# Moving a value projection and splitting norm steps inside context attention

## The chip, the cores and the metric

The kernel runs on one core of a Trainium2 chip. The metric is the device time of one execution in microseconds (us); lower is better. All numbers below are us unless marked otherwise.

## The reference

One transformer block on `x` (2 x 1024 tokens x 256) with a context of 2 x 154 tokens x 192, everything in float32:

```python
h = _layernorm(x, ln1_g, ln1_b)
x = _attention(h, h, sa_wq, sa_wk, sa_wv, sa_wo, sa_bo) + x
h = _layernorm(x, ln2_g, ln2_b)
x = _attention(h, cond_emb, ca_wq, ca_wk, ca_wv, ca_wo, ca_bo) + x
h = _layernorm(x, ln3_g, ln3_b)
p = h @ ff_w1 + ff_b1
a, gate = (p[..., :D_FF], p[..., D_FF:])
h = a * jax.nn.gelu(gate, approximate=False) @ ff_w2 + ff_b2
return h + x
```

Attention has 16 heads of 64. The change touches context attention (the second one) and the norms that run beside it: the second norm (`ln2`) of batch 1 and the third norm (`ln3`) of batch 0.

## The kernel before

The program is one stream of instructions for each engine, in an order written out by hand. Nothing reorders it: each engine takes its instructions as they were emitted, and semaphores join the engines.

The work has three stages: self attention, context attention, and the gated feed-forward layer. In context attention a **unit** is one pair of heads of one batch. There are 16, unit 0 to 15; 0 to 7 are batch 0. A unit's 1024 tokens are taken in three **slots**, of 3, 3 and 2 tiles of 128 tokens. The loop over `c` (48 values) walks through them; `ui, n = divmod(c, 3)` gives unit and slot.

Each slot does the following, in order:

- `cross_first`: the scores `sc` on TensorE (64-row tiles, since a head has 64 features), their maxima on VectorE (`neg`), then exponentials on ScalarE (`p`, with their sums in `den`).
- `flush(stores)` before the exponentials emits copies that were held back from the slot before. `flush(lates)` emits the reciprocal (`rden`, VectorE) and the weighting by it (`p`, GpSimdE) for the slot before.
- `cross_drain`: two 32x32 block transposes of the weights on VectorE (`pT_ca`), for the slot two back.
- The slot's own share. Slot 0 has the cross values `poc` of the unit two back (`cross_values`, 32-row tiles, into two banks of the pool `mm_tile` and two of `sum_tile`), and VectorE and ScalarE copy them out (`o_ca`). Slot 1 has the query projection `pq` of the next unit (`cross_queries`, two `mm_tile` banks, 64-row tiles; ScalarE copies `q_ca`). Slot 2 has the output projection: pieces `py` of two token tiles each, added into the residual `x` by VectorE. Most units have two pieces, one ahead of and one behind the norm step of that slot.

Each of the two pools has two banks, given out in turn. So the first `mm_tile` bank taken after a query projection is the one that the first of the two query copies frees.

**Context values.** Every second unit (2, 4, ... 14) projects the context values of its own and the next unit with `context_values`: `pv`, two matmuls of 96 rows, in the trace four passes. ScalarE copies the result to `own_v`. SP's queue then writes it to memory (`vd`) and reads it back in another layout (`v_ca`). The function `back` and the list `later`, of which two entries are emitted at the end of a slot, set when that happens. In the kernel before, `pv` is emitted in slot 1, behind the queries, in a `sum_tile` bank.

**Norms beside the attention.** `norm_beside(kind, b)` puts the steps of a norm in the list `side`; `run_work` takes at most one of them in a slot. A norm has four kinds of function: `stats` (VectorE, two instructions for each of the eight token tiles), `deviation` (GpSimdE, two small ones for a pair of tiles), `normalize` (one small VectorE instruction, `off`, and two on GpSimdE, `xn`), and `turn` (TensorE transposes into a bank `ph`, then stores of `hT` on VectorE). For the two norms here a step `k` takes two tiles:

```python
for fns, first in ((turn, 3), (stats, 0), (deviation, 1), (normalize, 2)):
    for i, fn in enumerate(fns):
        t = i if fns is stats else 2 * i + 1
        lag.setdefault(first + t // n, []).append((fn, fns is turn))
```

So with `n = 2` steps 0 to 2 hold no `turn`; step 3 holds the first `turn`, the second `normalize`, the third `deviation` and the last two `stats`; step 4 has no `stats`, step 5 no `deviation`, and step 6 the last `turn` alone. A step with a `turn` needs a bank, and `run_work` in context attention gives one in slot 2 only; the other steps may go in any slot. `norm_beside("ca", 1)` is called in slot 0 of unit 2, `norm_beside("ff", 0)` in slot 0 of unit 11. In the kernel before, steps 0, 1 and 2 therefore run in the three slots of units 2 and 11, and steps 3 to 6 in slot 2 of the four units that follow (3 to 6, and 12 to 15).

GpSimdE also adds biases (`ca_bo`) and, in the last units, sums of feed-forward weights (`w1s`, `wf`) in these slots.

Of the kernel before, what the change touches and what calls it, by code (L numbers as in the profile page):

```python
# [18 lines left out]
def tile_transformer_block(ctx: ExitStack, tc: tile.TileContext, a: dict, out: bass.AP):  # L19
# [4 lines left out]
    B, S, D = x.shape  # L24
# [73 lines left out]
    for n in names:  # L98
        k = n_of[n]
# [204 lines left out]
    def tile_order(kind):  # L304

        if kind == "ff":
            return list(range(NT))
        return [t for i in range(NT // 2) for t in (i, NT // 2 + i)]

    def narrow(kind, b):  # L310

        return kind == "sa" or kind == "ca" and b < B - 1
# [13 lines left out]
    def norm_beside(kind, b):  # L326

        after = {"sa": None, "ca": "sa", "ff": "ca"}[kind]
        stats, deviation, normalize, turn = norm_pieces(kind, b)
        n = 1 if narrow(kind, b) else 2
        lag = {}
# [4 lines that stand above are left out]
        for k in range(NT // n + 3):  # L339
            tiles = tile_order(kind)[k * n:(k + 1) * n]  # L340
            needs = [(after, b, half, t) for half in range(NQ) for t in tiles if after]

            def step(fns=lag[k]):
                done = [fn() for fn, _ in fns]
                return next((fn for fn in done if fn), None)

            side.append((any(turns for _, turns in lag[k]), needs, step))
        if not narrow(kind, b):
            side.append((False, (), lambda: add_biases(kind, b)))

# [129 lines left out]
    def out_order(kind):  # L480

        return [t for t in tile_order("ff" if kind == "ca" else "ca") if t % 2 == 0]
# [73 lines left out]
    side, lates = [], []  # L556
# [3 lines left out]
    def run(piece):  # L560
        done = piece()
        if done is not None:
            (adds if getattr(done, "adds", False) else stores).append(done)

    def flush(queue):
        for fn in queue:
            fn()
        queue.clear()

    def run_work(n, n_side, bank=None, n_sum=0):  # L570

        while n > 0 and work:
            n -= work[0].banks
            run(work.pop(0))
        for _ in range(min(n_side, len(side))):
            needs_bank, needs, fn = side[0]
            if needs_bank and not bank and n <= 0 or not added.issuperset(needs):  # L580
                break
            if needs_bank and not bank:
                n -= 1
            spare["bank"] = bank or mm_tile
            run(fn)
            side.pop(0)
        for i in range(min(max(n, 0) + n_sum, len(outs))):
            spare["out"] = mm_tile if i < n else sum_tile
            run(outs.pop(0))

    def out_pieces(kind, b, half, tiles):
        outs.extend(lambda t=t: out_piece(kind, b, half, t) for t in tiles)

    units = [(b, pr) for b in range(B) for pr in range(NPAIR)]
# [227 lines left out]
    def context_values(b, pr, bank=mm_tile):  # L822

        v = vs["ca", b, pr // 2] = pt_.tile([P, NB, VC], F32, tag="V", name=f"v_ca{b}_{pr}")
        pv = bank(f"pv_ca{b}_{pr}")
        for c in range(2):
            nc.tensor.matmul(
                pv[:, :VC], lhsT=ctxT[:, c, b * TP:b * TP + P],  # L830
                rhs=wsl["ca", pr, "v"][:, c, :], start=(c == 0), stop=(c == 1),
            )

        def store():
            own = one.tile([P, VC], F32, tag="own_v", name=f"own_v{b}_{pr}")
            nc.scalar.copy(own, pv[:, :VC])
            later.insert(0, lambda: nc.sync.dma_start(out=vd[b, pr][:P, :], in_=own))

            def back(a0):
                for a4 in range(a0, a0 + 2):  # L840
                    nc.sync.dma_start(
                        out=v[a4 * KB:(a4 + 1) * KB, :, :],
                        in_=vd[b, pr].rearrange("(n p) d -> p n d", p=KB))

            later.insert(2, lambda: back(0))
            later.insert(3, lambda: back(2))

        return store
# [367 lines left out]
    with tc.manual_schedule():  # L1216
# [61 lines left out]
        for p in range(SA):  # L1278
# [11 lines left out]
            ui, n = divmod(p, 2 * SH)  # L1290
# [26 lines left out]
        for c in range(CA):  # L1317
            if c == 0:
                pTc["ring"] = pt_.tile(
                    [P, 2 * NK, QH // 2], F32, tag="pT", name="pT_ca"  # L1320
                ).rearrange("p a b -> p (a b)")[:, :3 * 2 * NB * NT * KB].rearrange(
                    "p (u n j q) -> p u n j q", u=3, n=NB, j=2)
            if c == SH:
                out_pieces("sa", B - 1, NQ - 1, out_order("sa"))
                w1, w2, parts = hold_gated()
                add_biases("ca", 0)
                others = later[:] + [lambda: None] * (len(parts) - len(later))
                later[:] = [fn for pair in zip(parts, others) for fn in pair] + others[len(parts):]
            ui, n = divmod(c, len(CG))
            nxt = units[ui + 1] if ui + 1 < NU else None  # L1330
            if n == 0:
                cross_beside(ui)
            elif n == 1 and 1 <= ui < NU - 2:
                load_weights("ca", units[ui + 2][1], "q")
            elif n == 2 and nxt and ui:
                load_weights("ca", nxt[1], "v")
            flush(adds)
            between = None
            if c < 2:
                if c == 0:  # L1340
                    turn_group(SA - 3, 1)
                reciprocals(SA + c - 2)
                factors(SA + c - 2)
            then = cross_first(c)
            if c < 2:
                weighted(SA + c - 2, 0)
                weighted_beside(SA + c - 2, 1)
                if c == 0:
                    slot[SA - 1]["dd"] = differences(SA - 1, slot[SA - 1]["st"])
                    between = lambda: softmax_join(SA - 1)  # L1350
            flush(stores)
            flush(lates)
            if n == 0 and ui > 1:
                own, between = cross_values(ui - 2, [mm_tile] * 2 + [sum_tile] * 2)
                lates.append(then(between))
                own()
            else:
                lates.append(then(between))
            if c < 2:
                turn_group(SA + c - 2, 0)  # L1360
                turn_group(SA + c - 2, 1)
            cross_drain(c)
            if c == 0:
                run(lambda: self_values(2 * NU - 2, 1))
            elif c == 1:
                run(lambda: cross_queries(*units[2]))
            elif c in (2, 3):
                run(lambda: self_values(2 * NU - 1, c - 2))
            elif n == 0:
                run_work(0, 1)  # L1370
            elif n == 1:

                spare["turned"] = True
                if ui == 1 or not nxt:
                    run_work(2, 0)
                else:
                    run(lambda: cross_queries(*nxt))
                    if ui % 2 == 0:
                        run(lambda: context_values(*units[ui], sum_tile))
                run_work(0, 1)  # L1380
            else:
                run_work(0, 0, n_sum=1)
                flush(adds)
                run_work(0, 1, mm_tile)
                flush(stores)
                if ui > 1:
                    run_work(0, 0, n_sum=1)
                if ui and ui % HP == 0:
                    load_out("ca", *divmod(ui // HP - 1, NQ))
            if c == 0:  # L1390
                load_out("sa", B - 1, NQ - 1)
            for _ in range(min(2, len(later))):
                later.pop(0)()
            if c == CA - 16:
                weighted = [fn for n in range(4) for fn in weight_sums(n)]
            if CA - 16 <= c < CA - 4:
                weighted.pop(0)()
            elif c >= CA - 3:
                for n in {CA - 3: (4,), CA - 2: (5, 6), CA - 1: (7,)}[c]:
                    weight_sums(n)[0]()  # L1400
            if c == CA - 5:
                token_sums(0)
# [78 lines left out]
```

## Time and profile before

| | |
|---|---|
| median of 3 runs | 1078.59 (1078.13 to 1078.92) |
| the profiled execution | 1078.65, of which the span is 1076.9 |
| TensorE busy | 1065.6 of the span |
| VectorE, ScalarE, GpSimdE busy | 875.2, 651.0, 765.4 |

A row of a timeline gives the start in us from the span's start, the duration, the engine, the line of the kernel, the operation, what it writes and reads, tile sizes on TensorE (rows*columns), shapes, how many instructions were merged into the row, and in brackets the idle time before it with the engine that ended it. PE is TensorE's matmuls, PEld its weight loads, DVE VectorE, ACT ScalarE, POOL GpSimdE, SPq a queue of transfers. A float32 matmul of the program shows as two passes. Ends of matmuls are modelled, so the distance from one row's start to the next is a better measure than the duration. In a table of windows each line gives the stretch, its length, the busy time and instruction count of PE, PEld, DVE, ACT and POOL, then the granted clock of TensorE, the busy share of the transfer engines and their GB/s.

### The profile page before, as it was taken

Reading aid. Unit: us, or ns where it says so; the run is one execution under the profiler, and the core shown is the slowest. Engines: PE = TensorE matmul, PEld = TensorE weight load, DVE = VectorE, ACT = ScalarE, POOL = GpSimd, SP = SyncE. Lnnn points to the kernel's source line nnn. Section 1 sums busy time; section 2 is a strip of 40 time slices with the busy share of each in tenths; the row PEclk is TensorE's granted clock in tenths of the full one; section 3 lists DMA queues with packets and bytes.
Section 4 is the critical chain, followed back from the end, with each engine's and each line's share of the span. In section 5 each row is a group of like instructions: output and inputs, shape, how many; then the busy total and the mean of one; then the engine's idle time right before and its main releaser. Section 6 shows DMA issues by size and latency. Waiting matters only on the chain.

```text
span 1076.9 us, 45967 instructions
## 1 busy us (share of the span) xinstructions
PE 1065.6 (99%) x19060; PEld 712.3 (66%) x19060; DVE 875.2 (81%) x1283; ACT 651.0 (60%) x2081; POOL 765.4 (71%) x1600
## 2 busy tenths in 40 slices
PE   8999999999999999999999999999999999999998
PEld 6545657567565565566665655567766677788998
DVE  5789999998989989999989998978766777654554
ACT  5666767667666666666776666666566555242221
POOL 2677777778777787777777777768665687488774
PEclk9999999999999999999999999999999999999999
DMA  3232122111111111211211211135323221000000
GB/s 95 63 91 63 46 47 46 33 43 30 41 40 33 43 43 29 53 43 24 53 24 33 53 24 38 24 103 131 97 57 83 68 58 41 1 10 11 21 11 30
DMA packets 99234, 50.56 MB, mean 47 GB/s; under 512 B 30218, under 2 KB 97810, under 8 KB 99026
## 3 DMA queue, kind: packets, MB, share of 16 engines
q1 hardware_dynamic: 97698, 46.96, 18.0%
q8 instruction: 150, 2.46, 1.0%
q10 hardware_dynamic: 1328, 0.66, 0.2%
q14 instruction: 58, 0.48, 0.1%
HBM read 35.25 MB, written 3.41 MB: 36 GB/s over the span
## 4 chain that ended last, share of the span: by engine, by line
PE 91%; POOL 3%; DVE 2%; DMA 1%; ACT 1%; issue 1%; SPq 1%; DVEq 0%; POOLq 0%; ACTq 0%
PE s L493 19%; PE po L547 19%; PE py_sa L467 5%; PE py_ca L467 5%; PE pv_sa L393 5%; PE pq_ca L362 5%; PE pq_sa L362 5%; PE pk_sa L362 5%; PE sc L867 4%; PE poc L932 4%; PE pb L1037 3%; PE pf L1161 3%; PE pa L1037 2%; PE pc L1037 2%; PE pf L1200 1%; DMA st<-st 1%
## 5 line engine op out<-in xcount | busy, mean ns | idle before, releaser
L613 POOL TENSOR_SCALAR p<-p,rd,ee 128x512 f32<-128x512 f32 x508 | 387.4, 773 | 91.4 <-DVE rd L605 88.1
L508 ACT ACTIVATE p<-s,st 128x512 f32<-128x512 f32 x512 | 345.9, 687 | 175.5 <-DVE st L502 169.7
L502 DVE TENSOR_REDUCE st<-s 128x2 f32<-128x1024 f32 x256 | 308.8, 1207 | 51.1 <-issue 20.4
L640 DVE STREAM_TRANSPOSE pT<-p 128x1024 f32<-128x1024 f32 x256 | 302.4, 1219 | 1.5 <-POOL p L613 1.5
L493 PE MATMUL s<-k_sa,q_sa 64*32 64x512 f32 x4096 | 256.1, 591 | 2.4 <-ACT p L508 1.6
L547 PE MATMUL po<-pT,v_sa 64*32 64x256 f32 x8192 | 239.5, 376 | 0.9 <-ACT p L885 0.9
L547 PEld LDWEIGHTS po<-pT,v_sa 64*32 64x32 f32 x8192 | 177.5, 106 | 71.4 <-issue 26.2
L493 PEld LDWEIGHTS s<-k_sa,q_sa 64*32 64x32 f32 x4096 | 83.5, 106 | 101.0 <-issue 52.7
L885 ACT ACTIVATE p<-sc,neg 128x154 f32<-128x154 f32 x256 | 96.9, 401 | 74.9 <-DVE rden L893 74.4
L896 POOL TENSOR_SCALAR p<-p,rden 128x154 f32<-128x154 f32 x256 | 97.4, 402 | 61.7 <-DVE rden L893 61.2
L508 ACT ACTIVATION_READ_ACCUMULATOR p<-s,st 128x1 f32 x512 | 103.4, 202 | 0.0
L526 POOL TENSOR_TENSOR dd<-st 128x8 f32<-128x8 f32 x128 | 25.9, 202 | 73.5 <-DMA st<-st 69.7
L872 DVE TENSOR_REDUCE neg<-sc 128x6 f32<-128x924 f32 (+1 forms) x48 | 48.0, 1000 | 31.0 <-PE sc L867 30.9
L393 PEld LDWEIGHTS pv_sa<-sa_wv,hT_ln 64*128 64x128 f32 x1024 | 58.5, 188 | 14.2 <-issue 9.2
L393 PE MATMUL pv_sa<-sa_wv,hT_ln 64*128 64x128 f32 x1024 | 61.7, 275 | 0.0
L467 PE MATMUL py_ca<-ca_wo,o_ca 128*128 128x256 f32 x256 | 60.8, 385 | 0.0
L467 PE MATMUL py_sa<-sa_wo,o_sa 128*128 128x256 f32 x256 | 59.8, 386 | 0.0
L467 PEld LDWEIGHTS py_sa<-sa_wo,o_sa 128*128 128x128 f32 x256 | 47.2, 190 | 18.0 <-ACT v_sa L402 5.9
L362 PE MATMUL pq_ca<-hT_ln,ca_wq 64*128 64x512 f32 (+1 forms) x352 | 58.2, 589 | 0.0
L362 PE MATMUL pk_sa<-hT_ln,sa_wk 64*32 64x512 f32 x960 | 57.1, 590 | 0.0
L362 PE MATMUL pq_sa<-hT_ln,sa_wq 64*32 64x512 f32 (+1 forms) x976 | 56.7, 586 | 0.0
L885 ACT ACTIVATION_READ_ACCUMULATOR p<-sc,neg 128x1 f32 x256 | 55.3, 216 | 0.0
(132 smaller groups left out, 1442.6 us busy)
## 6 DMA issues: line engine op xcount, KB each, us to landing
v_sa<-v_sa SPq DMA_DIRECT2D x32, 256.0 KB, 3.8
st<-st SPq DMA_DIRECT2D x510, 1.0 KB, 1.8
v_ca<-vd SPq DMA_DIRECT2D x32, 160.0 KB, 3.1
sa_wq<-in_L_xattn_sa_wq_dram SPq DMA_DIRECT2D x32, 128.0 KB, 3.2
sa_wk<-in_L_xattn_sa_wk_dram SPq DMA_DIRECT2D x32, 128.0 KB, 3.2
sa_wv<-in_L_xattn_sa_wv_dram SPq DMA_DIRECT2D x32, 128.0 KB, 3.2
ca_wq<-in_L_xattn_ca_wq_dram SPq DMA_DIRECT2D x32, 128.0 KB, 3.4
wf<-in_L_xattn_ff_w_dram SPq DMA_DIRECT2D x12, 256.0 KB, 5.3
```

Source lines behind the costliest of these rows:

```text
L362: nc.tensor.matmul(pq[r][f:f + m, at:at + n], lhsT=wt[own, c, f:f + m], rhs=h[own, c, t0:t0 + n], start=(c == 0), stop=(c == NH - 1), tile ...
L393: nc.tensor.matmul(pv[r][:, i * P:(i + 1) * P], lhsT=h[own, c, i * P:(i + 1) * P], rhs=wt[own, c, :], start=(c == 0), stop=(c == NH - 1), ...
L467: nc.tensor.matmul(py[:, e * D:(e + 1) * D], lhsT=o[:, i, (t + e) * P:(t + e + 1) * P], rhs=wo[kind, b, g][:, i, :], start=(i == 0), stop= ...
L493: nc.tensor.matmul(sc[a4 * KB:(a4 + 1) * KB, j, :], lhsT=q[r, c:c + KB], rhs=k[r, h * HB:(h + 1) * HB], start=True, stop=True, tile_positi ...
L502: nc.vector.tensor_reduce(st[:, 0, 0, i, :], sc, AX.X, ALU.max, negate=True)
L508: nc.scalar.activation(pr[:, j, :], sc[:, j, :], AF.Exp, bias=st[:, 0, 0, i, j:j + 1], accum_out=st[:, 0, 1, i, j:j + 1],)
L547: nc.tensor.matmul(po[a2][d:d + KB, :QH // 2], lhsT=v[r, t, e, d:d + KB], rhs=pT[r, d // DH * NK + n, :], start=(t == 0 and e == 0), stop= ...
L613: nc.gpsimd.tensor_scalar(pr[:, j, :], pr[:, j, :], v["rd"][:, c:c + 1], v["ee"][:, 0, c:c + 1], op0=ALU.mult, op1=ALU.mult,)
L640: nc.vector.transpose(halves[h][:, :, c:c + KB], slot[p]["members"][i].rearrange("p j (n k) -> p (j n) k", k=KB))
L885: nc.scalar.activation(pr_[:, j, i, :T], sc[:, j, i * T:(i + 1) * T], AF.Exp, bias=neg[:, j, i:i + 1], accum_out=den[:, j, i:i + 1],)
L896: nc.gpsimd.tensor_scalar(pr_[:, j, i, :T], pr_[:, j, i, :T], rden[:, j, i:i + 1], 1.0, op0=ALU.mult, op1=ALU.mult,)
L1037: nc.tensor.matmul(into[:, :BT], lhsT=lhs, rhs=wh[pair][i], start=first, stop=True, skip_group_check=True)
```

## The change

For the two norms named above each step with a `turn` is cut in two: the `turn` alone, and then the rest of the step as an entry of its own in `side`. The `turn` keeps slot 2; the rest, which needs no bank, is taken in the next slot, slot 0 of the following unit. The first step 3 now runs its `turn` in slot 2 of unit 3 (unit 12) and its `stats`, `deviation` and `normalize` in slot 0 of unit 4 (unit 13), and so on.

`context_values` is emitted in slot 2 of the same units, between the two output pieces and ahead of the `turn`, in an `mm_tile` bank; before it was in slot 1, in a `sum_tile` bank. Its copy to `own_v` is emitted at the end of slot 2, behind that slot's exponentials on ScalarE; before it was ahead of them. The order of transfers on SP's queue is the same as before, and so are the number and kind of all instructions.

```diff
-            def step(fns=lag[k]):
+            def step(fns):
                 done = [fn() for fn, _ in fns]
                 return next((fn for fn in done if fn), None)

-            side.append((any(turns for _, turns in lag[k]), needs, step))
+            parts = [lag[k]]
+            if kind == "ca" and b == B - 1 or kind == "ff" and b < B - 1:
+                parts = [[f for f in lag[k] if f[1] == turns] for turns in (True, False)]
+            for fns in parts:
+                if fns:
+                    side.append(
+                        (any(turns for _, turns in fns), needs, lambda fns=fns: step(fns)))
...
                 else:
                     run(lambda: cross_queries(*nxt))
-                    if ui % 2 == 0:
-                        run(lambda: context_values(*units[ui], sum_tile))
                 run_work(0, 1)
             else:
                 run_work(0, 0, n_sum=1)
                 flush(adds)
+                if ui and ui % 2 == 0:
+                    run(lambda: context_values(*units[ui]))
                 run_work(0, 1, mm_tile)
                 flush(stores)
                 if ui > 1:
```

## Prediction

> **What bounds the kernel now.** I read the page first, then a table of windows over the context-attention stage, cut where each unit's cross values (`poc`) start, then the timelines of TensorE, VectorE, ScalarE and GpSimdE inside it.
>
> ```profile
> span 1076.9 us, 45967 instructions
> PE 1065.6 (99%) x19060; PEld 712.3 (66%) x19060; DVE 875.2 (81%) x1283; ACT 651.0 (60%) x2081; POOL 765.4 (71%) x1600
> PE 91%; POOL 3%; DVE 2%; DMA 1%; ACT 1%; issue 1%; SPq 1%; DVEq 0%; POOLq 0%; ACTq 0%
> ```
>
> TensorE is busy for 99% of the span and carries 91% of the chain that ended last. A change counts only if it alters the sum of TensorE's steps or makes TensorE wait. All that the diff moves lies in units 2 to 14 of context attention. The windows (length, then PE, PEld, DVE, ACT and POOL busy) show what one unit costs:
>
> ```profile
> 740.28:753.14 12.86, 12.86 (x151) 9.72 (x149) 10.68 (x30) 7.89 (x38) 12.11 (x34) 1.00 0.98 228
> 753.14:767.42 14.28, 14.28 (x154) 9.71 (x152) 10.38 (x23) 8.05 (x37) 10.33 (x27) 1.00 0.19 53
> 767.42:779.79 12.37, 12.37 (x151) 8.80 (x149) 9.76 (x21) 7.69 (x36) 7.89 (x22) 1.00 0.59 154
> 779.79:793.41 13.62, 13.62 (x154) 9.38 (x153) 9.56 (x20) 8.07 (x37) 6.29 (x19) 1.00 0.16 45
> 793.41:805.33 11.92, 11.92 (x146) 8.40 (x144) 8.28 (x16) 7.72 (x36) 8.68 (x23) 1.00 0.37 79
> 805.33:818.52 13.19, 13.19 (x151) 9.00 (x149) 8.28 (x16) 8.07 (x37) 9.36 (x24) 1.00 0.14 42
> 869.80:882.46 12.66, 12.66 (x151) 9.13 (x149) 9.68 (x20) 7.68 (x36) 10.36 (x27) 1.00 0.27 67
> ```
>
> A plain unit (7) takes 11.92. With transposes (5) it is 12.37, with a value projection (8) 13.19, with both (6) 13.62. So the projection costs 1.27 (13.19 - 11.92) or 1.25 (13.62 - 12.37), the transposes 0.45. Units 3, 4 and 13 exceed their kind by 0.49, 0.66 and 0.29: those are waits.
>
> **The projection, moved.** TensorE in unit 6, and in unit 5, which has no projection:
>
> ```profile
> 783.02 3.60 PE L362 MATMUL pq_ca<-hT_ln,ca_wq 64*128 64x512 f32 x16
> 786.55 1.13 PE L829 MATMUL pv_ca<-ca_wv,ctxT 96*128 96x256 f32 x4
> 787.61 0.80 PE L867 MATMUL sc<-kT,q_ca 64*128 64x154 f32 x8
> 788.33 1.99 PE L467 MATMUL py_ca<-ca_wo,o_ca 128*128 128x256 f32 x8
> 790.16 0.60 PE L280 MATMUL ph_ln<-ident,xn_ln 128*128 128x128 f32 x4
> 790.60 1.89 PE L467 MATMUL py_ca<-ca_wo,o_ca 128*128 128x256 f32 x8
> 792.42 1.06 PE L867 MATMUL sc<-kT,q_ca 64*128 64x154 f32 x12
> ```
> ```profile
> 770.66 3.60 PE L362 MATMUL pq_ca<-hT_ln,ca_wq 64*128 64x512 f32 x16
> 774.09 0.69 PE L867 MATMUL sc<-kT,q_ca 64*128 64x154 f32 x8
> 774.71 1.99 PE L467 MATMUL py_ca<-ca_wo,o_ca 128*128 128x256 f32 x8
> 776.54 0.60 PE L280 MATMUL ph_ln<-ident,xn_ln 128*128 128x128 f32 x4
> ```
>
> Today `pv` stands between queries and scores, both in 64-row tiles, and itself uses 96 rows. From start to start, queries to the next step take 3.53 with `pv` behind them and 3.43 without; `pv` takes 1.06; scores to output tile take 0.72 behind it and 0.62 without. That adds up to 1.26, as the windows say. How much of it is matmul? Eight passes of 256 columns take 1.83 in `py`, which is also entered from 64 rows.
>
> ```profile
> 786.55 0.73 PEld L829 LDWEIGHTS pv_ca<-ca_wv,ctxT 96*128 96x128 f32 x4 [0.76 <-DVE pT_ca L912]
> 789.95 0.57 PEld L280 LDWEIGHTS ph_ln<-ident,xn_ln 128*128 128x128 f32 x4
> L829 PE MATMUL pv_ca<-ca_wv,ctxT x32: 379/379/483, 693.3 to 890.0; 96*128 96x256 f32 x32
> L467 PE MATMUL py_ca<-ca_wo,o_ca x256: 379/379/483, 748.1 to 930.7; 128*128 128x256 f32 x128
> ```
>
> Both operations have passes of 379 ns and first ones of 483 (a pass overlaps the next, so these are not pitches). The excess of 0.10 is a weight load in the open: the first load of `pv` starts with its matmul at 786.55, while that of `ph`, between two 128-row groups, starts 0.21 ahead of its matmul. One pass is therefore (1.83 - 0.10) / 8 = 0.216, four are 0.86, and about 0.4 of `pv` is the price of leaving 64-row tiles and coming back. Between the two output tiles nothing is left and come back to. The transposes already there prove it: 0.44 in the timeline (790.16 to 790.60), 0.45 in the windows, no surcharge. Saving: 1.27 - 0.86 = 0.41 in three units without transposes (2, 8, 10) and 1.25 - 0.86 = 0.39 in four with them (4, 6, 12, 14), together **2.8**.
>
> The trace has no 96-row pass next to a 128-row one. If 96 against 128 costs as much as 96 against 64, the saving is 0; if it costs nothing, 2.8, or 2.9 at most. I take 2.8, because `pv` and `py` have the same durations, first passes included, and differ only in unused rows. The Trainium skill (TensorEngine Tiling (Array Packing), Key Properties and Available Configurations) says that a change of tiling mode drains TensorE, and lists row tilings of 128, 64 and 32 only. By it 96 rows would run as the 128-row mode and the sum would be 2.8; no run here shows that.
>
> What is queued behind the moved `pv`: transposes, second output tile, next scores, cross values. Its new wait is for the bank of the first query copy. In unit 5 the two copies start at 4.41 after the queries (row below), so the first is done at 4.96; `pv` would come at 774.71 - 770.66 + 1.83 = 5.88. Cover 0.9: no cost in units 6 to 14. On ScalarE the copy of `pv` now stands behind four exponentials, 1.5 us later (below), and its bank is next wanted by `poc`, which starts 10.4 after the queries (793.41 - 783.02); in unit 5's rhythm the copy is done by about 7.4 (4.41 + 1.1 + 1.5 + 0.4). On SP's queue the write of `own_v` and all behind it (value read-backs, query weights) wait as much longer; values are needed two units later, weights one, so nothing shows.
>
> **The norm steps, moved.** Before, statistics, deviation and normalization ran in slot 2 with the transposes. In unit 3:
>
> ```profile
> 750.70 0.42 DVE L240 BATCH_NORM_STATS2 st_ln<-x 128x6 f32<-128x256 f32 x1
> 751.82 1.36 DVE L291 TENSOR_SCALAR hT_ln<-ph_ln,cols 128x128 f32<-128x128 f32 x4
> 753.10 0.68 DVE L474 TENSOR_TENSOR x<-py_ca,x 128x512 f32<-128x512 f32 x1
> 753.14 3.08 PE L932 MATMUL poc<-pT_ca,v_ca 32*64 32x256 f32 x80
> ```
>
> Statistics and offset take 1.12 on VectorE (750.70 to 751.82) ahead of the transposes' stores and the add that frees a bank for `poc`. The add ends at 753.78, 0.64 after `poc` starts. That is unit 4's excess of 0.66, and unit 13 loses its 0.29 the same way. After the change that VectorE work starts after `poc`, so both go: **0.95**. The statistics of tiles still ahead of any transpose (units 2 and 11) do not move, nor do their waits.
>
> They come back in slot 0, in front of the maxima of slot 1. Unit 2 shows today what that does:
>
> ```profile
> 732.05 3.60 PE L362 MATMUL pq_ca<-hT_ln,ca_wq 64*128 64x512 f32 x16
> 733.07 0.39 DVE L240 BATCH_NORM_STATS2 st_ln<-x 128x6 f32<-128x256 f32 x1
> 734.11 1.08 DVE L872 TENSOR_REDUCE neg<-sc 128x6 f32<-128x924 f32 x1
> 735.31 0.39 ACT L885 ACTIVATE p<-sc,neg 128x154 f32<-128x154 f32 x1 [2.24 <-DVE rden L893]
> 737.52 1.11 ACT L377 ACTIVATE q_ca<-pq_ca 128x512 f32<-128x512 f32 x2
> 738.47 0.41 ACT L836 COPY own_v<-pv_ca 128x256 f32<-128x256 f32 x1
> 743.48 0.65 ACT L943 COPY o_ca<-poc 128x256 f32<-128x256 f32 x2
> 743.51 3.67 PE L362 MATMUL pq_ca<-hT_ln,ca_wq 64*128 64x512 f32 x15
> ```
> ```profile
> 771.67 1.08 DVE L872 TENSOR_REDUCE neg<-sc 128x6 f32<-128x924 f32 x1
> 775.07 1.11 ACT L377 ACTIVATE q_ca<-pq_ca 128x512 f32<-128x512 f32 x2
> 772.94 2.28 POOL L896 TENSOR_SCALAR p<-p,rden 128x154 f32<-128x154 f32 x6 [2.50 <-DVE rden L893]
> ```
>
> With statistics in front, the maxima start 2.06 after the queries (734.11 - 732.05) instead of 1.01, the query copies at 5.47, and the first copy is done at 6.02. What takes that bank waits: `pv` in unit 4, the transposes in unit 13, due at 5.88. With the offset op as well I put each at 0.3, **0.6 lost**. The near end is 0, if ScalarE catches up; the far end 0.85 each, if the bank is that of the second copy, 0.55 later.
>
> Unit 2 loses cover too. Its `pv` waits 0.15 (6.02 against 5.88), and the copy of `pv` moves behind four exponentials at 0.37 each (2.21 / 6 from 735.31 to 737.52): 738.47 + 1.48 + 0.41 = 740.36. With one output tile only, `poc` is due near 738.1 + 0.86 + 0.99 = 739.95 (0.99 for the scores, 792.42 to 793.41) and needs that bank: 0.41. TensorE then comes so late that unit 3's wait of 0.49 (half of the queries at 743.51 needs a bank that the `poc` copies from 743.48 free) should vanish. Net **0.1 lost**.
>
> GpSimdE's share in slot 0 is two small ops and two normalizations, about 2 us. They fit the 2.50 that it idles there before the weighting at 772.94; where weight sums share the slot, the weighting slips some 0.6, within VectorE's slack. In the units with `pv` or transposes alone, nothing else is late.
>
> Sum: 2.8 + 0.95 - 0.6 - 0.1 = 3.05, say **3.0**. The profiled execution took 1078.65, of which 1076.9 is span, and the median is 1078.59: 1078.59 - 3.0 = **1075.6**.
>
> **Rivals.**
> 1. *96 rows against 128 is a switch of its own.* `pv` then pays 0.2 on either side and saves nothing; the moved steps leave 0.95 - 0.7 = 0.25. Time 1078.3. For it: no neighbouring rows; against it: equal passes. Chance 0.16.
> 2. *The weight load was hidden anyway, so the place of `pv` does not matter.* Also 1078.3. Against it stands the load at 786.55, not ahead of its matmul. The Trainium skill (TensorE: Matmul & The Clock Gate, Step-by-step) says that the queue pulls weight loads ahead of matmuls in flight when row groups do not conflict; here that is seen at 789.95 and not at 786.55. Chance 0.05.
> 3. *Slower: the moved `pv` waits for the query copies in every unit.* It decides from a copy 0.9 later than in unit 5's rows; each 0.1 beyond costs 0.7 over seven units. To end above 1078.59 the wait must reach 3.0 / 7 = 0.43 a unit, copies 1.35 late; at 1.7 late the time is 1081. For it: unit 2's copies are 1.06 late where statistics stand in slot 0. Against it: only units 2 and 4 have both. Chance 0.08.
>
> **Numbers.** A measurement of this kernel tells some 0.2% (2.2 us) from no change. The forecast, with 0.71, spans 1074.2 (no new waits and unit 3's wait gone: 2.9 + 0.95 + 0.49, so 4.3) to 1076.4. Towards the first rival, half a switch gives 1.4 + 0.25, or 1076.9, and the range reaches 1077.6 to leave out no more than 2 in 10. Faster 0.71; same 0.20 (rivals 1 and 2, nearly all); slower 0.09.
>
> **What would show it.** In the changed profile the plain unit with `pv` should take 12.78 (11.92 + 0.86), with both 13.23; `pv` should have no first pass of 483 and its first load should start ahead of its matmul. The `poc` group of unit 4 should shrink by 0.66 from 3.08, that of unit 13 by 0.29. A short wait ahead of `pv` should appear in units 2 and 4 and ahead of the transposes in unit 13. I am wrong if the units with `pv` keep 13.19, or if TensorE waits ahead of `pv` in unit after unit.

## Result and the profile after

The changed kernel takes 1076.02 (median of 13 runs, 1074.73 to 1077.59) against 1078.37 before (median of 13, 1077.53 to 1079.63): 2.35 less, ratio 0.9977 with a 95% interval of 0.9969 to 0.9985. The profiled execution after is the slowest of its 13, with 1077.59 and a span of 1075.8. So the spans of the two profiles (1076.9 and 1075.8) differ by 1.1 only, and the stage of context attention has to be read by itself.

Windows over the whole stretch from unit 2's `poc` to the first `poc` of the feed-forward stage, of before and then of after (length, then busy time and instruction count of PE, PEld, DVE, ACT, POOL):

```profile
728.82:907.88 179.06, 179.06 (x2059) 125.75 (x2057) 132.95 (x288) 109.49 (x509) 128.15 (x336) 1.00 0.31 78
```
```profile
730.57:906.81 176.24, 175.73 (x2059) 125.16 (x2057) 133.24 (x288) 109.05 (x509) 126.88 (x334) 1.00 0.32 79
```

The stage is 2.82 shorter. It also begins 1.75 later (730.57 against 728.82), behind a self-attention stage that the diff does not touch. In the waits of TensorE over the whole span, the one of the self-attention scores for the exponentials is 3.1 in 7 waits after and 1.6 in 3 waits before (each line below gives the total, the count and the longest):

```profile
PE s L499 <- ACT p L514: 3.1, 7, 1.1
```
```profile
PE s L493 <- ACT p L508: 1.6, 3, 1.1
```

Over all eight kernels profiled here the stage begins anywhere from 727.15 to 730.57, so this belongs to the execution and not to the change. Behind the stage 169.0 of the span are left in both profiles; 1.75 later, 2.82 shorter and an equal rest make up the 1.1. Below, "the stage" is the stretch above, and its length is what I compare. No kernel was profiled twice, but units that two kernels have in common agree in it to 0.02.

The same units as in the prediction, from the windows of after (units 3, 4, 5, 6, 7, 8 and 13):

```profile
742.00:754.54 12.54, 12.54 (x151) 8.84 (x149) 9.94 (x23) 7.81 (x37) 11.30 (x31) 1.00 0.90 208
754.54:768.19 13.65, 13.49 (x154) 9.47 (x152) 10.90 (x25) 7.96 (x37) 9.60 (x25) 1.00 0.19 47
768.19:780.55 12.36, 12.36 (x150) 8.79 (x148) 9.63 (x21) 7.72 (x36) 8.24 (x23) 1.00 0.74 198
780.55:793.78 13.23, 13.23 (x154) 9.55 (x152) 9.72 (x21) 7.98 (x37) 7.33 (x21) 1.00 0.04 13
793.78:805.71 11.93, 11.93 (x147) 8.41 (x145) 8.28 (x16) 7.71 (x36) 8.68 (x23) 1.00 0.53 117
805.71:818.50 12.79, 12.79 (x151) 9.15 (x149) 8.28 (x16) 8.03 (x37) 9.29 (x24) 1.00 0.14 43
868.98:881.78 12.80, 12.55 (x150) 8.71 (x148) 10.43 (x23) 7.69 (x36) 9.66 (x26) 1.00 0.45 108
```

Units with a projection fell from 13.62 to 13.23 and from 13.19 to 12.79. Units without one kept 11.92 and 12.36. Unit 3 fell by 0.32, unit 4 by 0.63, and unit 13 rose, from 12.66 to 12.80.

TensorE in unit 6, then its weight loads there:

```profile
783.79 3.60 PE L368 MATMUL pq_ca<-hT_ln,ca_wq 64*128 64x512 f32 x16
787.22 0.69 PE L873 MATMUL sc<-kT,q_ca 64*128 64x154 f32 x8
787.84 1.99 PE L473 MATMUL py_ca<-ca_wo,o_ca 128*128 128x256 f32 x8
789.67 1.03 PE L835 MATMUL pv_ca<-ca_wv,ctxT 96*128 96x256 f32 x4
790.54 0.60 PE L280 MATMUL ph_ln<-ident,xn_ln 128*128 128x128 f32 x4
790.98 1.89 PE L473 MATMUL py_ca<-ca_wo,o_ca 128*128 128x256 f32 x8
```
```profile
787.84 1.59 PEld L473 LDWEIGHTS py_ca<-ca_wo,o_ca 128*128 128x128 f32 x8 [0.16 <-issue]
789.46 0.84 PEld L835 LDWEIGHTS pv_ca<-ca_wv,ctxT 96*128 96x128 f32 x4
```

From start to start `pv` takes 0.87 (789.67 to 790.54), scores 0.62. The first weight load of `pv` now starts 0.21 ahead of its matmul (789.46 against 789.67), as that of `ph` did before, and its four passes take 377 to 381 ns in this unit: the first pass of 483 is gone, as the prediction said. (In units 2 and 4, below, it is still there.)

The `poc` groups that waited in the kernel before are short: unit 4's (754.54) and unit 13's (868.98) both reach the next scores after 2.34. The waits that came in their place, from TensorE's timeline in units 2, 3, 4 and 13 (the `poc` at 742.00 opens unit 3):

```profile
737.86 1.99 PE L473 MATMUL py_sa<-sa_wo,o_sa 128*128 128x256 f32 x8
739.95 1.13 PE L835 MATMUL pv_ca<-ca_wv,ctxT 96*128 96x256 f32 x4
...
742.00 2.59 PE L938 MATMUL poc<-pT_ca,v_ca 32*64 32x256 f32 x80
744.52 1.06 PE L873 MATMUL sc<-kT,q_ca 64*128 64x154 f32 x12
...
761.82 1.99 PE L473 MATMUL py_ca<-ca_wo,o_ca 128*128 128x256 f32 x8
763.98 1.13 PE L835 MATMUL pv_ca<-ca_wv,ctxT 96*128 96x256 f32 x4 [0.16 <-ACT q_ca L383]
764.95 0.60 PE L280 MATMUL ph_ln<-ident,xn_ln 128*128 128x128 f32 x4
...
876.26 1.99 PE L473 MATMUL py_ca<-ca_wo,o_ca 128*128 128x256 f32 x8
878.51 0.63 PE L280 MATMUL ph_ln<-ident,xn_ln 128*128 128x128 f32 x4 [0.25 <-ACT q_ca L383]
```

The next group comes 2.09 after the start of `py` in unit 2, 2.16 in unit 4 and 2.25 in unit 13. Without a wait (unit 6) it comes after 1.83. So it is 0.26, 0.33 and 0.42 late from start to start; the profile counts from modelled ends and prints nothing, 0.16 and 0.25 in these rows. The weight loads of `pv` in units 2 and 4 name the releaser and start with their matmuls, not ahead of them:

```profile
739.95 0.73 PEld L835 LDWEIGHTS pv_ca<-ca_wv,ctxT 96*128 96x128 f32 x4 [0.50 <-ACT q_ca L383]
763.98 0.73 PEld L835 LDWEIGHTS pv_ca<-ca_wv,ctxT 96*128 96x128 f32 x4 [0.56 <-ACT q_ca L383]
```

So in both units `pv` also pays its late first load again: 0.97 to the transposes in unit 4 instead of 0.87, and 1.06 to the scores in unit 2, where 0.95 is measured without a wait (in the experiment "The first statistics later"). In unit 3 the `poc` takes 2.52 to the scores behind it, 0.17 more than in unit 4 (754.54 to 756.88 in the same timeline, 2.34). The copy `own_v`, which by the prediction's account frees a bank that it needs, ends at 742.13, after the start of `poc`; the profile names no releaser there.

The maxima and the query copies of unit 4, which has statistics in slot 0, and then of unit 6, which has none:

```profile
759.87 1.12 DVE L878 TENSOR_REDUCE neg<-sc 128x6 f32<-128x924 f32 x1
763.30 1.11 ACT L383 ACTIVATE q_ca<-pq_ca 128x512 f32<-128x512 f32 x2
```
```profile
784.84 1.11 DVE L878 TENSOR_REDUCE neg<-sc 128x6 f32<-128x924 f32 x1
788.27 1.11 ACT L383 ACTIVATE q_ca<-pq_ca 128x512 f32<-128x512 f32 x2
```

From the start of the queries (757.77 and 783.79) the maxima come after 2.10 against 1.05, and the copies after 5.53 against 4.48. In unit 13 the copies come after 5.54. Its transposes were not held up by their input: the normalized tile was finished at 875.58, and they start at 878.51.

Units 2 together with 3, before and after:

```profile
728.82:740.28 11.46, 11.46 (x143) 7.47 (x141) 9.75 (x24) 7.88 (x37) 8.16 (x22) 1.00 0.05 15
```
```profile
730.57:742.00 11.43, 11.33 (x143) 7.56 (x141) 10.04 (x26) 7.85 (x37) 8.11 (x22) 1.00 0.01 4
```

With unit 3's 12.86 and 12.54 that is 24.32 before and 23.97 after.

### The profile page after: what moved, and what is told of

It is laid out like the page before. It is cut to its first block, busy times and chain, and to the rows that moved or that the text cites. A ratio compares the mean times of both kernels' runs of the same rounds, so it can differ in the third digit from the quotient of the medians.

```text
span 1075.8 us, 45966 instructions
## 1 busy us (share of the span) xinstructions
PE 1062.7 (99%) x19060; PEld 706.1 (66%) x19060; DVE 875.1 (81%) x1283; ACT 650.4 (60%) x2081; POOL 762.3 (71%) x1600
## 4 chain that ended last, share of the span: by engine, by line
PE 84%; DVE 4%; POOL 3%; DMA 3%; ACT 3%; SPq 1%; issue 1%; DVEq 0%; POOLq 0%; ACTq 0%
PE s L499 18%; PE po L553 17%; PE py_sa L473 5%; PE py_ca L473 5%; PE pv_sa L399 5%; PE pk_sa L368 4%; PE pq_sa L368 4%; PE pq_ca L368 4%; PE poc L938 4%; PE pb L1043 3%; PE pf L1167 3%; PE sc L873 3%; DMA st<-st 3%; PE pa L1043 2%; PE pc L1043 2%; POOL p L619 1%
```

## Experiments

Six kernels, each profiled and timed beside the kernel before. The first expectations say that the stage ends at unit 15's `poc`; their lengths, such as 179.06, are those of the stretch above, which ends one `poc` later.

**Projection alone.** The cut of the norm steps is taken out of the changed kernel.

```diff
-            if kind == "ca" and b == B - 1 or kind == "ff" and b < B - 1:
-                parts = [[f for f in lag[k] if f[1] == turns] for turns in (True, False)]
```

> Only the projection is moved; the norm steps stay whole, in slot 2. Stage means the time from the start of unit 2's poc to the start of unit 15's poc in the profile: 179.06 before, 176.24 after the whole change. Theory: the projection alone brings all of the gain and the cut of the norm steps nothing on balance. Units 6, 8, 10, 12, 14 save 0.40 each, unit 4 too (its poc wait of 0.66 stays), units 2 and 3 save 0.35 together as after the change, and unit 13's wait of 0.29 goes without any cut, because the projection now gives VectorE 0.86 more between unit 12's two output tiles. Stage 176.0, about 0.2 shorter than with the whole change; time about 1075.7. Rival, as the prediction had it (the cut is worth 0.24 on balance): unit 13 keeps its 0.29, stage 176.5.

Ratio 0.9973 (0.9962 to 0.9983), median 1075.52. Windows: the stage, and units 4 and 13:

```profile
727.15:903.16 176.01, 175.92 (x2059) 125.66 (x2057) 132.87 (x288) 109.07 (x509) 127.56 (x336) 1.00 0.32 80
751.10:764.99 13.89, 13.89 (x155) 9.88 (x153) 10.48 (x23) 8.07 (x37) 10.83 (x27) 1.00 0.16 45
865.77:878.13 12.36, 12.36 (x150) 8.80 (x149) 9.25 (x19) 7.68 (x36) 9.66 (x26) 1.00 0.45 113
```

The stage is 3.05 shorter than before, 0.23 shorter than with the whole change. Unit 13 has lost its wait without any cut. VectorE in unit 12 shows why:

```profile
862.46 0.42 DVE L240 BATCH_NORM_STATS2 st_ln<-x 128x6 f32<-128x256 f32 x1
...
863.59 0.99 DVE L291 TENSOR_SCALAR hT_ln<-ph_ln,cols 128x256 f32<-128x256 f32 x2
864.89 0.69 DVE L478 TENSOR_TENSOR x<-py_ca,x 128x512 f32<-128x512 f32 x1 [0.32 <-PE py_ca L471]
```

The statistics still stand ahead of the stores and the add. But `pv` puts off the second output tile by 0.86, so VectorE is done early and idles 0.32 before the add. The rival stage of 176.5 did not come.

**Cut alone.** The projection is put back where it was.

```diff
                     run(lambda: cross_queries(*nxt))
+                    if ui % 2 == 0:
+                        run(lambda: context_values(*units[ui], sum_tile))
...
-                if ui and ui % 2 == 0:
-                    run(lambda: context_values(*units[ui]))
```

> Only the norm steps are cut; the projection stays in slot 1 behind the queries. Theory: unit 4 loses its poc wait and pays nothing for it, since the projection in slot 1 covers the query copies: 14.28 becomes 13.62. Unit 13 swaps 0.29 for the wait of 0.42 ahead of its transposes: 12.80. All other units as before. Stage 178.5 against 179.06 before; time 1077.8, not to be told from no change. Rival (the cut brings the larger part of the gain): stage 177 or less, units with a projection shorter than 13.62 and 13.19.

Ratio 0.9993 (0.9984 to 1.0002), median 1077.96: not to be told from no change. Stage and units 4 and 13:

```profile
730.10:908.61 178.51, 178.27 (x2058) 124.95 (x2056) 132.76 (x288) 109.23 (x509) 126.87 (x334) 1.00 0.32 78
754.40:768.03 13.63, 13.63 (x155) 9.39 (x153) 10.61 (x25) 7.95 (x37) 9.60 (x25) 1.00 0.13 36
870.40:883.19 12.79, 12.55 (x150) 8.71 (x148) 10.42 (x23) 7.68 (x36) 9.66 (x26) 1.00 0.27 65
```

The cut brings 0.55 by itself, nearly all of it 0.65 in unit 4, minus 0.13 in unit 13, where the wait for the query copy outweighs the one that went. Alone, the parts bring 3.05 and 0.55, together 2.82. They are not additive, since the projection's move removes one of the two waits that the cut is for, and takes away the cover for what the cut puts off in unit 4.

**The projection's passes twice, in the kernel before.** The second time writes the same values over the first.

```diff
-        for c in range(2):
+        for c in (0, 1, 0, 1):
             nc.tensor.matmul(
                 pv[:, :VC], lhsT=ctxT[:, c, b * TP:b * TP + P],
```

> The kernel before with the four passes of every context-value projection done twice, in the same place and bank (the second time overwrites the first with the same values). It asks whether the 1.27 of a projection is 0.86 of passes and a fixed 0.41 for leaving the 64-row tiles and coming back. Theory: 0.86 more in each of seven units, units with projection 14.05 (plain) and 14.48 (with transposes), stage 185.1, time 1084.4. Rival (passes of 96 rows between 64-row groups are slow in themselves): 1.27 more each, 14.46 and 14.89, stage 188, time 1087.3.

Ratio 1.0057 (1.0039 to 1.0076), median 1084.98. Stage, and units 6 and 8:

```profile
729.39:914.46 185.07, 185.07 (x2086) 130.99 (x2084) 132.80 (x288) 110.24 (x509) 128.09 (x336) 1.00 0.30 76
782.07:796.55 14.48, 14.48 (x158) 10.14 (x156) 9.56 (x20) 8.18 (x37) 6.28 (x19) 1.00 0.09 28
808.48:822.52 14.04, 14.04 (x154) 9.75 (x152) 8.28 (x16) 8.18 (x37) 9.35 (x24) 1.00 0.12 40
```

Four more passes cost 0.86 (13.62 to 14.48) and 0.85, where the first four cost 1.25 and 1.27. So about 0.4 is a fixed price for each time that TensorE leaves the 64-row tiles and returns.

**Statistics in slot 1.** The changed kernel with steps cut by kind, one entry of `side` for a slot (empty ones keep the beat): transposes in slot 2, deviation and normalization in slot 0, statistics in slot 1. The two norms start in slot 2 of unit 1 and slot 1 of unit 10.

```diff
...
+        entry([turn[0]], True)                 # slot 2
+        other(2, 1)                            # slot 0: deviation, normalize
+        statistics(3)                          # slot 1
+        entry([turn[1]], True)
...
+            if c == 2 * len(CG) - 1:
+                norm_beside("ca", B - 1)
+            if c == 10 * len(CG) + 1:
+                norm_beside("ff", 0)
```

> The whole change, with one more cut: transposes in slot 2, deviation and normalization in slot 0, statistics in slot 1, where VectorE idles 1.2 to 2.8 ahead of the maxima of slot 2. To make room the ln2 norm of batch 1 starts in slot 2 of unit 1 (one slot earlier) and the ln3 norm of batch 0 in slot 1 of unit 10 (two slots earlier). Theory: the waits left after the change are all made by statistics in slots 0 and 2: 0.53 in unit 2, 0.43 in unit 4, 0.61 in unit 12, 0.43 in unit 13. All go: units 4, 6, 12, 14 take 13.23, unit 2 takes 11.05, 3, 5 and 13 take 12.37, stage 174.2, time 1074. Rival (statistics in slot 1 push back the maxima of slot 2 and all behind them, so the wait only moves): stage about 176, new waits ahead of poc in units 3, 5, 12 and 14.

Ratio 0.9957 (0.9944 to 0.9969), median 1074.11. Stage, and units 2, 4, 12 and 13:

```profile
728.12:902.73 174.61, 174.61 (x2059) 125.89 (x2057) 133.04 (x288) 109.05 (x509) 127.33 (x333) 1.00 0.32 80
728.12:739.58 11.46, 11.46 (x143) 8.34 (x141) 9.29 (x23) 8.11 (x37) 9.83 (x27) 1.00 0.01 3
751.94:765.17 13.23, 13.23 (x154) 9.56 (x153) 10.70 (x25) 7.96 (x37) 9.64 (x25) 1.00 0.17 43
852.11:865.34 13.23, 13.23 (x154) 9.55 (x152) 10.33 (x23) 7.96 (x37) 10.33 (x26) 1.00 0.04 12
865.34:877.70 12.36, 12.36 (x150) 8.79 (x148) 10.24 (x23) 7.69 (x36) 10.29 (x26) 1.00 0.44 113
```

Units 4, 12 and 13 are free of waits. Unit 2 is not: 11.46 instead of 11.05. Its row on TensorE shows where:

```profile
731.36 3.99 PE L419 MATMUL pq_ca<-hT_ln,ca_wq 64*128 64x512 f32 x16
```

The queries take 3.99 instead of 3.60; one half runs late. Statistics in slot 2 of unit 1 hold up the maxima of unit 2's slot 0, the exponentials behind them, and the `poc` copies on ScalarE, of which one frees that half's bank:

```profile
731.22 0.65 ACT L1000 COPY o_ca<-poc 128x256 f32<-128x256 f32 x2
```

These copies start 3.10 after `poc`; in the next kernel, which moves the statistics, they start after 2.48 (731.94 against 729.46).

**The first statistics later.** The same kernel, with the first eight statistics instructions of the ln2 norm together in slot 1 of unit 2.

```diff
...
-            statistics(0)                      # 5
-            other(0, -1)                       # 6
-            statistics(1)                      # 7
-            none()                             # 8
+            entry(stats[:4], waits=needs(0) + needs(1))
+            other(0, -1)                       # 8
...
-            if c == 2 * len(CG) - 1:
+            if c == 2 * len(CG) + 1:
```

> Like the kernel with statistics in slot 1, with one difference: the ln2 norm of batch 1 no longer starts with statistics in slot 2 of unit 1. Its first eight statistics instructions stand together in slot 1 of unit 2, its first deviation in slot 2. Stage means the time from unit 2's poc to the first poc of the feed-forward stage: 179.06 before, 176.24 after the whole change, 174.61 with statistics in slot 1. Theory: the 0.39 that the queries of unit 2 still lost there came from statistics in slot 2 of unit 1, which put back the maxima of slot 0 and with them the poc copies on ScalarE that free the bank of the second half of the queries. With these statistics in slot 1 of unit 2 ScalarE is busy to 5.5 after the queries anyway, unit 2 takes 11.05 and the stage 174.2. Time about 1073.6. Rival (eight instructions at once, 2.1 us, are more than VectorE idles there): unit 2 or 3 loses 0.4 or more at another place, stage 174.6 or longer.

Ratio 0.9959 (0.9946 to 0.9971), median 1074.44. Stage and unit 2:

```profile
729.46:903.67 174.21, 174.21 (x2058) 125.18 (x2056) 133.22 (x288) 109.03 (x509) 126.80 (x334) 1.00 0.33 80
729.46:740.52 11.06, 11.06 (x143) 7.64 (x141) 9.43 (x23) 8.09 (x37) 8.40 (x24) 1.00 0.01 4
```

The wait is gone and every unit from 2 to 14 takes the time of its kind without a wait; the stage is 4.85 shorter than before. By times alone this kernel and the one ahead of it cannot be told apart: 0.33 is about a ninth of the spread of the runs (1072.39 to 1075.35).

**Cut for the ln2 norm only.** The projection is moved; `kind == "ff"` is taken out of the condition.

```diff
-            if kind == "ca" and b == B - 1 or kind == "ff" and b < B - 1:
+            if kind == "ca" and b == B - 1:
```

> The projection moved, and only the ln2 norm of batch 1 cut; the ln3 norm of batch 0 keeps whole steps in slot 2. Stage from unit 2's poc to the first poc of the feed-forward stage. Theory: the cut pays in unit 3 to 4 (13.65 against 13.89 with the projection alone), and costs in unit 13 (12.80 against 12.36), because unit 12's moved projection already gives VectorE the room; so this mixture keeps both good ends: stage 175.8, against 176.24 with both cut and 176.01 with none. Time about 1075.3. Rival (the two cuts act on each other, or only the slots of unit 2 count): stage as with both cut, 176.2.

Ratio 0.9967 (0.9955 to 0.9979), median 1074.80. Stage:

```profile
727.75:903.53 175.78, 175.53 (x2058) 125.18 (x2056) 132.95 (x288) 109.10 (x509) 127.48 (x336) 1.00 0.32 80
```

With the projection moved, the cut is worth 0.23 for the ln2 norm (176.01 to 175.78) and costs 0.46 for the ln3 norm (175.78 to 176.24).

## Why the prediction was right, point by point

*TensorE is the bound.* It held: every difference of the stage, in all seven kernels compared with before, is a sum of passes and of waits seen on TensorE.

*The projection saves 2.8.* It held, in size and mechanism. Unit 6 fell by 0.39 and unit 8 by 0.40; the forecast was 0.39 and 0.41. The open point, whether 96 rows next to 128 rows switch, is settled by rows: `pv` takes 0.87 from start to start between `py` and `ph`, with its first load ahead of its matmul. With that the first two rivals fall. The doubled passes show that the surcharge is fixed: here leaving the 64-row tiles and coming back cost 0.4. The rule of the Trainium skill (TensorEngine Tiling (Array Packing), Key Properties), that a change of tiling mode drains TensorE, agrees with this. The first weight load started ahead of its matmul from 128 to 96 rows (789.46) and with it from 64 to 96 (786.55). The pull-ahead of weight loads that the Trainium skill describes (TensorE: Matmul & The Clock Gate, Step-by-step) is seen in the first case and not in the second.

*The third rival, a wait for the query copies in every unit.* It came true in unit 2 (0.26) and in unit 4 (0.33), where statistics stand in slot 0, and in none of the five others. The cover of 0.9 was a little too large. The prediction took the first copy to be done after half of the merged row of two, 0.55; the two overlap, one takes 0.62, and `pv` comes 0.67 (unit 2) and 0.68 (unit 4) after the copies' start. That makes the cover about 0.8, and copies 1.06 and 1.12 later than in unit 5 of before then give the 0.26 and the 0.33.

*Removing 0.95 of waits.* Here a step was mis-sized. Both waits are gone, but beside the moved projection only unit 4's 0.66 needs the cut. Unit 13's 0.29 goes with the projection alone, because `pv` in front of the second output tile gives VectorE the time. The prediction priced the cut in the slots of before, not in those that the other half of the change makes. So where it forecast a net gain of about 0.25 for the cut, it is a loss of 0.23 on top of the move, and a gain of 0.55 without it.

*Losing 0.6 in units 4 and 13.* 0.43 each, 0.86 together: the mechanism was right (statistics ahead of the maxima of slot 1, late query copies, a bank), the size about a third short. Start to start the waits are 0.33 and 0.42, where each was put at 0.3, and left out was that in unit 4 a wait also lays the first weight load of `pv` open, 0.10.

*Losing 0.1 in units 2 and 3.* The sum held: units 2 and 3 together went from 24.32 to 23.97, 0.35 less, with 0.31 forecast (0.41 saved, 0.1 lost). Within it the terms were off in both directions, which is in part luck: `pv` waited 0.26 instead of 0.15 and paid 0.10 more for its first load, and `poc`, which so came later, lost 0.17 instead of 0.41. Unit 3's 0.49 vanished, as TensorE came late enough. The wait that the diff does not touch stayed: unit 12 has 0.61 of it, until statistics are moved to slot 1.

*The total.* Forecast 3.0, stage 2.82, medians 2.35 with an interval of about 1.6 to 3.3. That 0.29 was counted for the wrong half does not touch the sum. Its 3.05 differ from 2.82 by the 0.26 by which the two new waits were priced too low, less the 0.04 that units 2 and 3 brought in addition. The 0.5 between times and stage is less than the 3.4 by which the start of the stage varies from profile to profile; nothing here shows more about it.

## What to carry to other kernels

When TensorE is the bound, count how often it changes the height of its tiles. Here a group of 96 rows cost its passes plus a fixed 0.4 between groups of 64 rows, and its passes only between groups of 128 rows; other pairs of heights were not compared in this way. Price each half of a change in the schedule that the other half makes, not in the old one. Small steps on a helper engine belong in the slot in which that engine waits for the bound one; in front of what the bound engine's banks depend on, about a microsecond of them came back as 0.3 to 0.7 of waiting.

## What was not expected of the hardware

The first weight load of a group is left in the open not only by a change of tile height but also by a wait for a bank: `pv` took 0.97 to the next group in unit 4 against 0.87 in unit 6, and its load at 763.98 starts with its matmul. In unit 13, where it is the transposes that wait, this cost only 0.02 (0.46 to the next group against 0.44). And executions differ by up to 3.4 in when the stage begins (727.15 to 730.57, two kernels that are alike up to there), while units that two kernels share agree to 0.02. Why the self-attention stage varies was not examined.
